# Offsets on VectorE with an early first row, reordered norms and dots, and gate parts on GpSimd in an eight-stage graph and feed-forward kernel

## The chip, the cores and the metric

The kernel runs on one core of a Trainium2 chip. A core has five engines that work side by side, each through its own queue in order: TensorE (PE in the profile; PEld is its weight load), VectorE (DVE), ScalarE (ACT), GpSimd (POOL) and SyncE (SP), which here only issues DMA transfers. An engine waits for another by a semaphore, and whatever stands behind the waiting instruction in its queue waits too. The metric is the time of one execution on the device in microseconds (us); the figure is a median of several runs.

## The reference

`x` holds 625 nodes of 768 numbers. Eight stages each add something to it, four graph layers and four feed-forward layers in turn; every stage reads a layer norm of `x`:

```python
x = x + L0_gnn(layernorm(x))   # graph attention, 12 heads of 64
x = x + L0_ffn(layernorm(x))   # 8 experts, 2 per node, hidden size 192
x = x + L1_gnn(layernorm(x))   # normalised graph convolution
x = x + L1_ffn(layernorm(x))   # attention over all nodes, then 8 experts
x = x + L2_gnn(layernorm(x))   # two graph convolutions
x = x + L2_ffn(layernorm(x))   # soft mixture, 4 experts
x = x + L3_gnn(layernorm(x))   # two graph attention layers, 4 heads and 1
x = x + L3_ffn(layernorm(x))   # 8 experts, 2 per node
```

The attention of a graph layer is, for an edge from `s` to `d`:

```python
e = leaky_relu(a1[s] + a2[d], 0.2)
w = exp(e - max over the edges into d of e)
out[d] = sum(w * h[s]) / sum(w)
```

The first layer of L1_ffn's experts has biases, and its second layer too; all inputs and outputs are 32-bit floats.

## The kernel before

**Layout.** The nodes lie in five tiles of 125 (`NT`, `P`, `TILES`). `x` is kept with nodes on partitions; `xT` is its layer norm turned, features on partitions, in six chunks (`KD`). PSUM, TensorE's output memory, is one pool of four buffers of two banks (`ps`, line 89), through which every product and every transpose goes. The program is written in the order of the stages; the scheduler of the framework then sets each engine's queue, mostly in that order, and pulls later work ahead where it thinks that an engine would wait. So a line that is written later can stand earlier in a queue, and the profile tells which does.

**Strassen's way of multiplying.** Large products are cut into two by two blocks and made from seven products, with sums of blocks made before. `right_sums` (L421 to 439) makes four sums of the right matrix (L435 to L438, called T3, T2, T4 and T1), `left_sums` (L441) five of the left one on POOL, `tile_pair` (L462) runs the seven products for two node tiles, calling `between` after the first two. `half_nodes`, `half_begin` and `half_rest` do the same for the experts' first layer, where the halves are halves of the nodes.

**Norms.** `ln_tile` (L157) makes statistics on DVE (L167, L170), a square root on ACT (L171), a reciprocal (L172) and the scaling (L180) on DVE. `turn_tile` (L182) turns one tile with six transposes (L187) and copies it out on ACT, plainly (L191) or, for L1_ffn's two norms with weights, in six steps (L194). `final(t)` enters tile t's norm and marks it as due to be turned; `turn_due` turns what is due.

**Graph attention.** For each head, `gat_largest` (L553) spreads `a1` as a row over all partitions (L132, five transposes into one PSUM tile) and takes per node the largest over its edges, one DVE step for a tile (L560), with `mb` as mask; it then makes an offset `u` on POOL (L565 to L569). `gat_scores` (L539) makes the scores, on ACT (L547) and POOL (L551). `gat_exp` (L572) spreads `u` as a row, subtracts it from the whole score matrix on DVE (L582) and takes exponentials on ACT (L584). `gather` multiplies by the features (L118 in L0_gnn). `mask_tile` (L525) turns a tile of the counts and makes the mask. L0_gnn's loop (L873 to L902) runs over the heads as a pipeline: in round i the largest of head i, the exponentials of head i-2, `back` of head i-4, `gather` of head i-3 and the scores of head i. `score(i)` first copies head i-1's maxima with ACT (L813). The maxima and offsets have two buffers each (`gat_m`, `gat_u`).

**Experts.** `experts` (L967) runs the first layer in six blocks of two chunks (loop at L1088), and the gates beside it; `gate` (L1038) multiplies a chunk by its gate. In L1_ffn, `gate_parts` (L953) splits the gates into three 16-bit parts, seven DVE steps, needed by the products with the biases in the second layer. `down` (L1107) runs the second layer: tile 0 whole, then two pairs of tiles, t = 1 and t = 3, with the seven products in the order 1, 6, 7, 4, 2, 5, 3. The results of products 1, 6, 2 and 5 go into one PSUM tile (`a1`, `a2`), those of 7, 4 and 3 into another (`b1`, `b2`). After product 1 its result is copied by ACT (L1178) and the norm of tile 0 for the next stage is entered (L1183).

**Dots for a later stage.** L3_gnn needs its weight matrix times two vectors per head. `attention_vectors` (L1318) makes these beside L0_ffn and L1_ffn: each step loads a 128 by 512 piece (`av_w`, two buffers) and runs two DVE dot products (L1355), after a one-element copy (L1354) that puts them behind a given result. `experts` calls `beside(1, ...)` after each of five blocks (L1102), and `down` calls `beside(7, ...)` after the pair t = 1 (L1215): twelve in each of the two layers.

**Narrow products.** `narrow` (L257) multiplies by a few columns: small matmuls (L268), a copy by ACT (L273), five transposes back (L276) and a reduction on DVE (L277). L3_gnn calls it in its first layer's `second` (L2126) and before its second layer (L2191).

Of the kernel before, what the change touches and what calls it, by code (L numbers as in the profile page):

```python
# [9 lines left out]
F32 = mybir.dt.float32  # L10
# [25 lines left out]
class Net:  # L36
# [120 lines left out]
    def ln_tile(self, src, dst, scale=None, st=None, act=False):  # L157


        nc, sp = self.nc, self.small  # L160
        have = st is not None
        if not have:
            st = sp.tile([P, 12], F32, tag="lt_st", name="lt_st", bufs=3)
        mv = sp.tile([P, 2], F32, tag="lt_mv", name="lt_mv", bufs=3)
        rs = sp.tile([P, 1], F32, tag="lt_r", name="lt_r", bufs=3)
        for h in range(0 if have else 2):
            nc.vector.bn_stats(  # L167
                st[:, 6 * h : 6 * h + 6], src[:, h * (D // 2) : (h + 1) * (D // 2)]
            )
        nc.vector.bn_aggr(mv, st)  # L170
        nc.scalar.activation(rs, mv[:, 1:2], AF.Sqrt, bias=self.eps[:P])  # L171
        nc.vector.reciprocal(rs, rs)  # L172
        if scale is not None:
            nc.vector.tensor_tensor(rs, rs, scale, ALU.mult)
        if act:
            nb = sp.tile([P, 1], F32, tag="lt_n", name="lt_n")
            nc.vector.tensor_scalar(nb, mv[:, 0:1], rs, -1.0, ALU.mult, ALU.mult)
            nc.scalar.activation(dst, src, AF.Identity, bias=nb, scale=rs)
            return
        nc.vector.tensor_scalar(dst, src, mv[:, 0:1], rs, ALU.subtract, ALU.mult)  # L180

    def turn_tile(self, src, dst, t, scale=None, bias=None):  # L182
# [10 lines left out]
        for k in range(KD):  # L193
            nc.scalar.activation(  # L194
                dst[:, k, TILES[t]], pv[:, k, :P], AF.Identity,
                bias=bias[:, k : k + 1], scale=scale[:, k : k + 1],
            )
# [59 lines left out]
    def narrow(self, pool, chunks, w, cols, dst):  # L257


        nc, n, few = self.nc, len(chunks), w  # L260
# [13 lines left out]
        pv = self.nv(self.ps(), P, 128)  # L274
        for t in range(NT):
            nc.tensor.transpose(pv[:, t, :], hT[:, TILES[t]], self.ident)  # L276
        nc.vector.tensor_reduce(  # L277
            dst, pv.rearrange("p t (q e) -> p t e q", q=4)[:, :, 0:cols, :], AX.X, ALU.add
        )
# [141 lines left out]
    def right_sums(self, T, q, eng=None):  # L421
# [16 lines left out]
        eng.tensor_tensor(T1, B12, B11, ALU.subtract)  # L438
# [114 lines left out]
    def gat_largest(self, pool, mb, a1, a2):  # L553

        nc = self.nc
        row = self.spread(lambda t: a1[:, t : t + 1], P)
# [8 lines left out]
        nc.gpsimd.tensor_tensor(u, m, a2, ALU.add)  # L565
        v = self.small.tile([P, NT], F32, tag="gat_v", name="gat_v")
        nc.gpsimd.tensor_scalar(v, u, 0.8, 0.0, ALU.mult, ALU.max)
        nc.gpsimd.tensor_scalar(u, m, 0.2, None, ALU.mult)
        nc.gpsimd.tensor_tensor(u, u, v, ALU.add)  # L569
# [17 lines left out]
    def L0_gnn(self):  # L587
# [5 lines left out]
        with ExitStack() as ctx:  # L593
# [196 lines left out]
            for s in range(NT):  # L790
                self.log_counts(lc, s)
            for t in range(NT):
                self.mask_tile(mb, t, act=True)
# [79 lines left out]
            for i in range(H + 4):  # L873
                if i < H:
                    ms[i], us[i] = self.gat_largest(tmpp, mb, a1[i], a2[i])
# [77 lines left out]
    def gate_parts(self, gb, after):  # L953
# [4 lines left out]
        nc.vector.tensor_copy(r[:, 0, 0:1], after)  # L958
        parts = gb[:, :, 0, 0 : 3 * NEXP].rearrange("p t (e i) -> p t e i", i=3)
        nc.vector.tensor_copy(parts[:, :, :, 0], lg)  # L960
        nc.vector.tensor_tensor(r, lg, parts[:, :, :, 0], ALU.subtract)
        nc.vector.tensor_copy(parts[:, :, :, 1], r)
        nc.vector.tensor_tensor(parts[:, :, :, 2], r, parts[:, :, :, 1], ALU.subtract)
        for j in range(1, gb.shape[2]):
            nc.vector.tensor_copy(gb[:, :, j, 0 : 3 * NEXP], gb[:, :, 0, 0 : 3 * NEXP])

    def experts(self, over_all, w1, w2, gelu, b1=None, b2=None, after=None, beside=None):  # L967

        nc, tc, a, x = self.nc, self.tc, self.a, self.x
        with tc.tile_pool(name="moe", bufs=1) as big, ExitStack() as up_pool:  # L970
# [117 lines left out]
            for c in range(2, NF + 2, 2):  # L1088
# [12 lines left out]
                if beside and c < NF:  # L1101
                    beside(1, hg[:P, c + 1, 0:1])  # L1102
# [4 lines left out]
    def down(self, pool, w2, hg, gT, bias, after, beside):  # L1107
# [47 lines left out]
        for t in (1, 3):  # L1155
# [18 lines left out]
            )  # L1174
            U = pool.tile([P, 2, HD], F32, tag="U", name="U")
            U2, U3 = U[:, 0], U[:, 1]
            prod(1, a1)
            nc.scalar.copy(U2, a1)  # L1178
            add(x11, U2)
            prod(6, a2)  # L1180
            add(U2, U2, a2)
            if after and t == 1:
                self.final(0)  # L1183
            prod(7, b1)
            add(U3, U2, b1)
            add(x12, U2)
            prod(4, b2, (t + 1, bl))
# [12 lines left out]
            add(x22, U3)  # L1200
            prod(5, a2, (t + 1, br))
# [3 lines left out]
            add(x12, a2)  # L1205

# [7 lines left out]
            if beside and t == 1:  # L1214
                beside(7, U3[:, 0:1])  # L1215
# [179 lines left out]
    def L1_ffn(self):  # L1395
# [3 lines left out]
        with ExitStack() as ctx:  # L1399
# [31 lines left out]
            rights = self.right_sums(vp, columns(wv))  # L1431
# [570 lines left out]
    def L3_gnn(self):  # L2002
# [5 lines left out]
        with ExitStack() as ctx:  # L2008
# [23 lines left out]
            def project(h, *between):  # L2032
# [13 lines left out]
                for i, t in enumerate((1, 3)):  # L2046
                    if i < len(between):
                        between[i](T)
                    self.tile_pair(
                        T[:P, 3 * HK], lefts[t], rights,  # L2050
                        [hh[h][:, o, c, 0:HH] for o in (t, t + 1) for c in range(2)],
# [74 lines left out]
            def second(T):  # L2126
                self.turn_due(NT - 1)
                self.narrow(tp, [xT[:, k, :] for k in range(KD)], self.v1, 2 * H, ends)
                sums_of(3, None)
                for t in range(3, NT):  # L2130
                    self.mask_tile(mb, t)
# [59 lines left out]
            self.narrow(tp, chs, self.v2, 2, c)  # L2191
# [69 lines left out]
            prod(lambda t: A[t][0], B11, one, (1,))  # L2261
            self.gat_scores(w, c1, self.spread(lambda t: c2[:, t : t + 1], P), lc)
# [134 lines left out]
```

## Time and profile before

| what | us |
|---|---|
| median of 3 runs | 1891.52 (1891.14 to 1892.33) |
| the profiled execution, its own time | 1890.76 |
| its span, first to last instruction | 1889.0 |

| stretch, us from the start | stage | TensorE busy | DVE | ACT | POOL | granted clock |
|---|---|---|---|---|---|---|
| 0 to 90 | L0_gnn, counts of edges | 79.18 | 74.27 | 26.94 | 1.89 | 0.98 |
| 90 to 110 | L0_gnn, masks, first head | 11.98 | 14.89 | 14.89 | 10.63 | 0.74 |
| 110 to 225 | L0_gnn, heads | 96.29 | 103.14 | 99.33 | 94.00 | 0.86 |
| 303 to 344 | L0_ffn, second layer | 37.25 | 30.98 | 3.29 | 23.59 | 0.96 |
| 700 to 730 | L1_ffn, into the experts | 28.49 | 17.38 | 14.61 | 15.22 | 1.00 |
| 730 to 765 | L1_ffn, first layer of experts | 32.50 | 20.15 | 7.41 | 23.66 | 1.00 |
| 790 to 830 | L1_ffn, second layer | 36.57 | 31.74 | 3.04 | 23.59 | 1.00 |
| 1405 to 1452 | L3_gnn, first heads | 44.77 | 29.17 | 12.97 | 24.83 | 1.00 |

The profile comes from one execution. A line of its timeline reads: start in us, length in us, engine, line of the kernel, operation, the tile written and the tiles read with their shapes, how many were merged, and in brackets how long the engine had stood idle before it and what ended that. `128x384 f32` is partitions by elements; `L125` is the helper through which most matmuls go, so the tile names tell the product. Busy time of TensorE is modelled; idle time of an engine that nothing waits for costs nothing.

### The profile page before, as it was taken

How to read it: one execution, taken by the hardware profiler on the slowest of the kernel's cores; microseconds unless marked ns; L12 is line 12 of the kernel's file. 1: busy time of each engine (PE TensorE's matmuls, PEld its weight loads, DVE VectorE, ACT ScalarE, POOL GpSimd, SP SyncE). 2: the span in 40 equal slices, each digit the busy share in tenths (PEclk: the TensorE clock that was granted, in tenths of full speed). 3: DMA queues.
4: the chain of work that ended last, by engine and by line, in shares of the span. 5: the costliest groups of instructions: out<-in, count | busy, mean ns of one | idle time of the engine just before them, and what ended most of it. 6: DMA issues, size and time to landing. Idle time of an engine off the chain costs nothing.

```text
span 1889.0 us, 21692 instructions
## 1 busy us (share of the span) xinstructions
PE 1821.8 (96%) x8224; PEld 1270.4 (67%) x8224; DVE 1112.4 (59%) x2211; ACT 528.2 (28%) x963; POOL 658.4 (35%) x556
## 2 busy tenths in 40 slices
PE   8969899999999999999999999999999999999998
PEld 7844565555677766655555778878767888556765
DVE  8789856547566765674936464555756555144452
ACT  2479721002254533100110131322314233111200
POOL 0079665234410044743106322231235321401551
PEclk9968999999999999999999999999999999999999
DMA  2040142210200024414420211001011122021321
GB/s 70 22 145 34 40 116 70 78 58 27 92 25 26 1 70 153 127 53 140 138 67 34 76 43 59 26 26 34 6 39 35 40 72 67 1 73 52 94 72 33
DMA packets 69637, 115.03 MB, mean 61 GB/s; under 512 B 8189, under 2 KB 38111, under 8 KB 69534
## 3 DMA queue, kind: packets, MB, share of 16 engines
q1 hardware_dynamic: 69274, 113.57, 18.9%
q8 instruction: 65, 1.06, 0.2%
q14 instruction: 38, 0.31, 0.1%
q10 hardware_dynamic: 260, 0.09, 0.0%
HBM read 111.63 MB, written 2.01 MB: 60 GB/s over the span
## 4 chain that ended last, share of the span: by engine, by line
PE 84%; DVE 8%; ACT 2%; DMA 2%; issue 2%; POOL 1%; SPq 0%; ACTq 0%; DVEq 0%; POOLq 0%
PE ps L125 65%; PE ps L118 4%; PE ps L768 2%; PE ps L1889 2%; PE ps L1518 2%; PE ps L1550 2%; PE ps L1537 1%; PE ps L187 1%; POOL gat_w L551 1%; PE ps L132 1%; DVE gat_w L582 1%; PE ps L1735 1%; DMA x<-in_x 1%; PE ps L706 1%; DVE av_junk L1355 1%
## 5 line engine op out<-in xcount | busy, mean ns | idle before, releaser
L327 POOL TENSOR_TENSOR S<-w 128x384 f32<-128x384 f32 x40 | 41.4, 1040 | 401.9 <-PE ps L125 298.9
L125 PE MATMUL ps<-xT,w 128*128 128x313 f32 x480 | 137.6, 427 | 0.7 <-ACT pr L1526 0.7
L125 PE MATMUL ps<-w,xT 128*125 128x384 f32 (+2 forms) x392 | 125.2, 473 | 0.0
L125 PE MATMUL ps<-T,w 128*128 128x313 f32 x408 | 122.0, 430 | 0.9 <-DVE U L401 0.9
L551 POOL TENSOR_TENSOR gat_w<-gat_w,xT 125x625 f32<-125x625 f32 x60 | 86.2, 1469 | 102.8 <-DVE xT L523 96.5
L125 PEld LDWEIGHTS ps<-xT,w 128*128 128x128 f32 x480 | 89.3, 189 | 33.6 <-ACT pr L1526 0.9
L125 PE MATMUL ps<-T,S 128*128 128x313 f32 x348 | 103.8, 432 | 1.7 <-DVE T L307 1.4
L125 PEld LDWEIGHTS ps<-w,xT 128*125 128x125 f32 x392 | 72.8, 188 | 46.2 <-issue 11.1
L125 PE MATMUL ps<-xT,S 128*128 128x313 f32 x336 | 100.9, 429 | 2.1 <-DVE hg L401 2.1
L125 PE MATMUL ps<-w,S 128*125 128x384 f32 x292 | 99.8, 487 | 2.6 <-DVE x L1170 2.6
L125 PEld LDWEIGHTS ps<-T,w 128*128 128x128 f32 x408 | 75.6, 189 | 32.2 <-issue 1.8
L125 PE MATMUL ps<-w,hg 128*125 128x384 f32 x288 | 96.3, 486 | 0.0
L125 PE MATMUL ps<-hh,gat_w 125*125 125x257 f32 (+1 forms) x400 | 89.8, 379 | 0.0
L125 PE MATMUL ps<-w,x2T 128*125 128x384 f32 (+1 forms) x280 | 84.2, 449 | 0.0
L125 PEld LDWEIGHTS ps<-T,S 128*128 128x128 f32 x348 | 64.0, 189 | 28.7 <-ACT lt L355 4.4
L125 PEld LDWEIGHTS ps<-w,S 128*125 128x125 f32 x292 | 54.5, 188 | 42.4 <-DVE x L1170 3.9
L125 PEld LDWEIGHTS ps<-hh,gat_w 125*125 125x125 f32 x400 | 73.4, 187 | 11.3 <-issue 0.4
L125 PEld LDWEIGHTS ps<-xT,S 128*128 128x128 f32 x336 | 62.1, 189 | 26.6 <-POOL hg L1041 2.5
L118 PE MATMUL ps<-gat_w,ft 125*65 125x500 f32 (+1 forms) x240 | 74.9, 471 | 4.4 <-DVE gat_w L582 3.1
L125 PEld LDWEIGHTS ps<-w,hg 128*125 128x125 f32 x288 | 53.6, 188 | 36.6 <-issue 0.6
L1355 DVE CUSTOM_DVE_ANT_0 av_junk<-av_w,av_a 128x512 f32<-128x512 f32 (+1 forms) x80 | 74.1, 926 | 6.4 <-DMA av_w<-in_L_gnn_W 4.1
L560 DVE CUSTOM_DVE_ANT_0 junk<-ps,mb 125x625 f32<-125x625 f32 x85 | 68.5, 806 | 13.9 <-PE ps L132 9.9
(459 smaller groups left out, 3794.7 us busy)
## 6 DMA issues: line engine op xcount, KB each, us to landing
w<-in_L_ffn_phiT SPq DMA_DIRECT2D x8, 1536.0 KB
w<-in_L_gnn_W SPq DMA_DIRECT2D x8, 1536.0 KB
gate<-gD SPq DMA_DIRECT2D x24, 312.5 KB
w<-in_L_ffn_w SPq DMA_DIRECT2D x6, 1152.0 KB
w<-in_L_gnn_W SPq DMA_DIRECT2D x6, 1152.0 KB
av_w<-in_L_gnn_W SPq DMA_DIRECT2D x24, 256.0 KB
av_w<-in_L_gnn_W SPq DMA_DIRECT2D x16, 384.0 KB
w<-in_L_ffn_w SPq DMA_DIRECT2D x3, 1536.0 KB
```

What stands on the lines that cost most here:

```text
L118: self.nc.tensor.matmul(pv[:, s, :], lhs[i], rhs[i][:, s, :], start=i == 0, stop=i == n - 1)
L125: self.nc.tensor.matmul(out, lhs[i], rhs[i], start=i == 0, stop=i == n - 1)
L132: self.nc.tensor.transpose(pv[:, t, :], col(t).to_broadcast([P, rows]), self.ident[:P, :P])
L187: nc.tensor.transpose(pv[:, k, :P], src[:, k * 128 : (k + 1) * 128], self.ident[:P, :P])
L327: nc.gpsimd.tensor_tensor(S1, A21, A22, ALU.add)
L551: nc.gpsimd.tensor_tensor(w[:, s, :], w[:, s, :], lc[:, s, :], ALU.add)
L560: nc.vector.tensor_tensor_reduce(self.n3(junk), row, self.n3(mb[:, t, :]), 1.0, -3e38, ALU.subtract, ALU.max, m[:, t : t + 1],)
L768: nc.tensor.matmul(acc[j // 2][:, j % 2, :], ohs[:, TILES[j]], ohd[:, 0:HN], start=c == cs[0], stop=c == cs[-1],)
L1355: nc.vector.tensor_tensor_reduce(junk, wt, row, 1.0, 0.0, ALU.mult, ALU.add, dst)
L1518: nc.tensor.matmul(sv[r][:, s, :], qk[half[r], 0, TILES[t]], self.n3(qk[half[r], 1, :])[:, s, :], start=True, stop=True,)
L1550: nc.tensor.matmul(ov[half[r]], v[:, s, h * DH : (h + 1) * DH], pT[r][:, s, :], start=s == 0, stop=s == NT - 1,)
L1889: nc.tensor.matmul(pv[:, j, :], zTs[t][:, k, :], w2[k // 3][:, k % 3, js], start=k == 0, stop=False,)
```

## The change

Several small edits are made together. (1) The offset `u` is made by two DVE steps in place of four on POOL, in all 17 heads: `0.2 m + max(0.8 (m + a2), 0)` becomes the equal `max(0.2 m, m + 0.8 a2)`. (2) In L0_gnn the row for head 0 is spread before the masks. (3) In `down`, two one-column ACT copies put the square root of tile 0's norm behind the copy of product 1. (4) The seven dots steps after the pair t = 1 are dealt out: two more among the first layer's blocks, one at the end of the pair t = 1, four in the pair t = 3. (5) `gate_parts` goes from DVE to POOL. (6) The last sum of L1_ffn's value weights goes to POOL. (7) When the last tile is turned with weights, every second chunk is written by DVE. (8) The transposes of both narrow products, and the two last masks of L3_gnn, move behind matmuls.

```diff
 def ln_tile(...)
         nc.vector.bn_aggr(mv, st)
+        if behind is not None:
+            nc.scalar.copy(rs, behind)
         nc.scalar.activation(rs, mv[:, 1:2], AF.Sqrt, bias=self.eps[:P])
 def turn_tile(...)
         for k in range(KD):
+            if t == NT - 1 and k % 2:
+                nc.vector.tensor_scalar(
+                    dst[:, k, TILES[t]], pv[:, k, :P], scale[:, k : k + 1], bias[:, k : k + 1],
+                    ALU.mult, ALU.add,
+                )
+                continue
 def narrow(...)
-        pv = self.nv(self.ps(), P, 128)
-        for t in range(NT):
-            nc.tensor.transpose(pv[:, t, :], hT[:, TILES[t]], self.ident)
-        nc.vector.tensor_reduce(
-            dst, pv.rearrange("p t (q e) -> p t e q", q=4)[:, :, 0:cols, :], AX.X, ALU.add
-        )
+        def turned():
+            pv = self.nv(self.ps(), P, 128)
+            for t in range(NT):
+                nc.tensor.transpose(pv[:, t, :], hT[:, TILES[t]], self.ident)
+            nc.vector.tensor_reduce(
+                dst, pv.rearrange("p t (q e) -> p t e q", q=4)[:, :, 0:cols, :], AX.X, ALU.add
+            )
+        return turned
 def right_sums(self, T, q, eng=None, last=None)
-        eng.tensor_tensor(T1, B12, B11, ALU.subtract)
+        (last or eng).tensor_tensor(T1, B12, B11, ALU.subtract)
 def gat_largest(self, pool, mb, a1, a2, row=None)
-        row = self.spread(lambda t: a1[:, t : t + 1], P)
+        if row is None:
+            row = self.spread(lambda t: a1[:, t : t + 1], P)
...
-        nc.gpsimd.tensor_tensor(u, m, a2, ALU.add)
-        v = self.small.tile([P, NT], F32, tag="gat_v", name="gat_v")
-        nc.gpsimd.tensor_scalar(v, u, 0.8, 0.0, ALU.mult, ALU.max)
-        nc.gpsimd.tensor_scalar(u, m, 0.2, None, ALU.mult)
-        nc.gpsimd.tensor_tensor(u, u, v, ALU.add)
+        nc.vector.scalar_tensor_tensor(u, a2, 0.8, m, ALU.mult, ALU.add)
+        nc.vector.scalar_tensor_tensor(u, m, 0.2, u, ALU.mult, ALU.max)
 def L0_gnn(self)
             for s in range(NT):
                 self.log_counts(lc, s)
+            row = self.spread(lambda t: al[:, t, 0, 0:1], P)
             for t in range(NT):
                 self.mask_tile(mb, t, act=True)
...
-                    ms[i], us[i] = self.gat_largest(tmpp, mb, a1[i], a2[i])
+                    ms[i], us[i] = self.gat_largest(
+                        tmpp, mb, a1[i], a2[i], None if i else row
+                    )
 def gate_parts(self, gb, after)
-        nc.vector.tensor_copy(r[:, 0, 0:1], after)
+        nc.gpsimd.tensor_copy(r[:, 0, 0:1], after)
...
 def experts(...)
                 if beside and c < NF:
-                    beside(1, hg[:P, c + 1, 0:1])
+                    beside(2 if c in (4, 8) else 1, hg[:P, c + 1, 0:1])
 def down(...)
+            def dots(n, after):
+                if beside and n in ((5,) if t == 1 else (1, 2, 3, 4)):
+                    beside(1, after[:, 0:1])
             prod(1, a1)
             nc.scalar.copy(U2, a1)
+            if after and t == 1:
+                nc.scalar.copy(U3[:, 0:1], U2[:, 0:1])
             add(x11, U2)
+            dots(1, x11)
             prod(6, a2)
             add(U2, U2, a2)
+            dots(2, U2)
             if after and t == 1:
-                self.final(0)
+                self.final(0, behind=U3[:, 0:1])
             prod(7, b1)
             add(U3, U2, b1)
             add(x12, U2)
+            dots(3, x12)
...
             add(x22, U3)
+            dots(4, x22)
             prod(5, a2, (t + 1, br))
             add(x22, a2)
...
             add(x12, a2)
+            dots(5, x12)
...
-            if beside and t == 1:
-                beside(7, U3[:, 0:1])
 def L1_ffn(self)
-            rights = self.right_sums(vp, columns(wv))
+            rights = self.right_sums(vp, columns(wv), last=nc.gpsimd)
 def L3_gnn(self)
                 for i, t in enumerate((1, 3)):
+                    behind = None
                     if i < len(between):
-                        between[i](T)
+                        behind = between[i](T)
                     self.tile_pair(
                         T[:P, 3 * HK], lefts[t], rights,
-                        [hh[h][:, o, c, 0:HH] for o in (t, t + 1) for c in range(2)],
+                        [hh[h][:, o, c, 0:HH] for o in (t, t + 1) for c in range(2)], behind,
                     )
...
             def second(T):
                 self.turn_due(NT - 1)
-                self.narrow(tp, [xT[:, k, :] for k in range(KD)], self.v1, 2 * H, ends)
+                turned = self.narrow(tp, [xT[:, k, :] for k in range(KD)], self.v1, 2 * H, ends)
                 sums_of(3, None)
-                for t in range(3, NT):
-                    self.mask_tile(mb, t)
+                def behind():
+                    turned()
+                    for t in range(3, NT):
+                        self.mask_tile(mb, t)
+                return behind
...
-            self.narrow(tp, chs, self.v2, 2, c)
+            turned = self.narrow(tp, chs, self.v2, 2, c)
...
             prod(lambda t: A[t][0], B11, one, (1,))
+            turned()
             self.gat_scores(w, c1, self.spread(lambda t: c2[:, t : t + 1], P), lc)
```

## The prediction, made before the changed kernel was run

> **What bounds the kernel now.** I read the page's first part, then the chain of waits, then TensorE's own waits, then the timeline around each of those.
>
> ```profile
> PE 1821.8 (96%) x8224; PEld 1270.4 (67%) x8224; DVE 1112.4 (59%) x2211; ACT 528.2 (28%) x963; POOL 658.4 (35%) x556
> ...
> PE 84%; DVE 8%; ACT 2%; DMA 2%; issue 2%; POOL 1%; SPq 0%; ACTq 0%; DVEq 0%; POOLq 0%
> ```
>
> TensorE is busy 1821.8 of 1889.0 us and carries 84% of the chain. The change removes no matmul, so it can only win out of the 67.2 us in which TensorE stands. Who it stands for (engine, line, waited for: us in total, times, longest):
>
> ```profile
> PE ps L132 <- POOL gat_u L569: 10.1, 3, 6.2
> PE ps L125 <- ACT U L1178: 5.0, 2, 2.6
> ...
> PE ps L125 <- DVE x L1170: 2.6, 2, 1.5
> ...
> PE ps L125 <- DVE hg L401: 2.1, 1, 2.1
> PE ps L276 <- ACT narrow L273: 1.6, 2, 0.8
> PE ps L125 <- DVE T L307: 1.4, 3, 0.9
> ...
> PE ps L187 <- DVE xn L180: 1.3, 1, 1.3
> ```
>
> From L0_ffn on TensorE is nearly full, so a wait taken from it there is time taken off. L0_gnn (90 to 225 us) is different: TensorE is busy 108.3 of 135 us and four engines hand work round; a wait of TensorE there is worth something only if the loop behind it gets shorter. I cost each part at its own place.
>
> **First head of L0_gnn (row spread ahead of the masks, offsets on DVE).** Timeline:
>
> ```profile
> 99.11 9.50 POOL L551 TENSOR_TENSOR gat_w<-gat_w,xT 125x625 f32<-125x625 f32 x5 [96.53 <-DVE xT L523]
> ...
> 109.52 0.20 POOL L569 TENSOR_TENSOR gat_u<-gat_u,gat_v 125x5 f32<-125x5 f32 x1
> ...
> 111.26 3.41 DVE L582 TENSOR_TENSOR gat_w<-gat_w,ps 125x3125 f32<-125x3125 f32 x1 [0.95 <-POOL gat_w L551]
> ```
>
> The four little POOL steps of head 0 (L565 to L569, 108.58 to 109.72) wait behind five L551; then TensorE spreads them (1.37) and L582 starts. The maxima (L560) start at 103.84 because the row is spread after the five masks. With the row first, each maximum waits only for its mask: ACT makes them every 1.37 us, the last at 105.6, so the fifth maximum ends at about 106.5. Two DVE steps of 5 columns cost about 0.35 (L844, also 125x5, is 0.19 long and lets the next start after 0.11). Spread done by 108.5; then L582 waits only for POOL's L551, 108.6. Start 108.75 instead of 111.26: **-2.5**. ACT's exp, the later rows and the gathers hang on L582, so they come along. The masks lose one of four PSUM buffers to the row; mask 3 then waits for ACT's release of mask 0 (100.9) and ACT reaches it only at 103.48: nothing.
>
> **Offsets in the other heads.** One head lasts 8.70 us (L582 at 159.05, 167.75, 176.45), in a ring:
>
> ```profile
> 166.02 0.78 PE L132 MATMUL ps<-ident,gat_u 125*125 125x125 f32 x5 [1.30 <-DVE gat_m L560]
> ...
> 166.70 0.18 ACT L813 COPY gat_w<-gat_m 125x5 f32<-125x5 f32 x1
> ...
> 167.01 0.81 DVE L560 CUSTOM_DVE_ANT_0 junk<-ps,mb 125x625 f32<-125x625 f32 x1 [0.56 <-POOL gat_u L565]
> ...
> 167.75 3.40 DVE L582 TENSOR_TENSOR gat_w<-gat_w,ps 125x3125 f32<-125x3125 f32 x1
> ```
>
> ACT's exps, L826, L813, one maximum, L582, exps again. POOL's offsets are not in it, so taking four steps (1.1 us) off POOL gains nothing. But `gat_u` has two buffers: the offset of head i overwrites that of head i-2, just read by the spread at 166.02. POOL could wait for that; now DVE waits, with L560 and L582 queued behind it and ACT's exps behind those. Behind L582 the two steps are free; between L560 and L582 they add 0.35 in each of some ten heads. The 0.56 idle lies in front and swallows part: I take **+0.8**, ends -1 (where POOL's late offset held a spread, as at 126.28) and +3.5.
> Can TensorE itself get faster here? The granted clock is 0.86 over 110 to 225 us: 20 gather matmuls take 7.18 at 119.77, after a stall of 6.2, and 5.43 in later heads. The Trainium skill ("TensorE: Matmul & The Clock Gate", Part 1) says that the clock halves after about 3.4 us of idleness, so a stall pushed below that would give 1.7 more. But the first stall goes from 6.2 to about 5 (from 109.9, when the first spread and the next row are out, to 115, when head 1's offset is there), still cold by the rule; I count 0.
>
> **Norm of tile 0 in both down-products.** Timeline of L0_ffn:
>
> ```profile
> 320.71 0.81 PE L125 MATMUL ps<-Td,hg 128*125 128x384 f32 x2
> ...
> 323.24 0.29 ACT L171 ACTIVATE lt_r<-lt_mv,eps 125x1 f32<-125x1 f32 x1 [18.50 <-DVE lt_mv L170]
> ...
> 323.63 0.48 ACT L1178 COPY U<-ps 125x384 f32<-125x384 f32 x1
> ...
> 324.17 5.83 PE L125 MATMUL ps<-Td,S 128*125 128x384 f32 x12 [2.64 <-ACT U L1178]
> ```
>
> The first product ends at 320.7; its copy could run at once, but ACT's queue has the norm's square root (L171) in front, which waits for DVE. TensorE stands 2.64 (and 2.31 in L1_ffn). The two one-column copies force the square root behind the L1178 copy: copy at 320.9, done at 321.4, when TensorE has just done its two filler matmuls. The price is two ACT copies of 0.19 (as L906), with nothing behind them but the norm of a tile turned 9 us later. Next late would be T2 and S2, ready by 313.5 and 311. **-4.5** of 4.95.
>
> **Dots.** Seven pairs (one 0.14 copy, two of 0.77) leave the end of pair t=1. There they ran with DMA waits of 1.18 and 1.38 in DVE's queue, and TensorE stood 1.53 (344.42) and 1.12 (829.31) for an L1170 sum behind them: **-2.4** of 2.65. Four now run in t=3, each behind a sum with a product of 3.9 us before the next read is due; DVE is idle 15 us between 356 and 380. Each has two `av_w` buffers and some 8 us for a 256 KB load; SP's queue sends the next stage's weights after them, so that load moves from 355.0 to about 362, needed at 379.7. Two more pairs per FFN go among the up-products at c = 4 and 8. There TensorE already stood 0.46 and 0.42 for a sum wedged between dots: cost 0 if they fit into DVE's gaps (2.2 us per block), 1.5 each if not; **+0.6** in all, ends 0 and 6.
>
> **L1_ffn.** (1) The fourth subtraction of the value weights goes to POOL. L438 took 1.34 at 459.14, ahead of the last tile's norm, and TensorE waited 1.28 for its xn at 463.77: **-1.2**. On POOL it costs about 2.7 (1.77 for 768 columns at L435, times 1.5), in a queue idle from 458.8 to 463.7; its product starts at 468.3. DVE may pay too: L180, the norm's scaling, took 1.10 beside a POOL step at 458.11 and 0.68 without one. A rule speaks against the move: the Trainium skill ("SBUF — State Buffer", SBUF: two separate sides) has DVE and GpSimd share a port pair that one of them holds for a whole instruction. By the rule L180 could wait the full 2.7, and the part would lose 1.4; by the row it loses 0.4 at most. POOL is through at 461.5, before the last L180 is due (461.7): I keep -1.2. (2) Half of tile 4's affine turn on DVE: six ACT steps take 2.19 at 722.74, then the T sums wait and TensorE 0.87. Three on each engine take 1.1: **-0.9**; at 464.6 nothing waits for it. (3) The gates' parts: DVE's five steps, L961 to L965, held L401 from 748.29 to 751.30 (L961 alone 1.49 for 40 columns), and TensorE stood 2.05 at 751.91: **-1.9**. POOL pays about 2.2 for seven steps of 0.2 to 0.4 (L1054, L567), where it has gaps of 2.05 and 1.09; behind them stand the gate multiplications, and sums used 11 us later.
>
> **L3_gnn.** Both narrow products' transposes move behind matmuls, so their ACT copy (0.83 and 0.80) is covered. The second now has DVE's reduction (0.2 and its hand-over) straight before the spread that reads it: -0.8 and -0.4. The offset at 1450.42 waits no more: -0.5. Masks 3 and 4 come 2.6 later and hold the logarithms (ACT L522, 1426.7 to 1429), which have until 1435: +0.2. **-1.5**.
>
> **Sum.** -2.5 + 0.8 - 4.5 - 2.4 + 0.6 - 1.2 - 0.9 - 1.9 - 1.5 = **-13.5 us**. The profiled execution took 1890.76 (span 1889.0, 1.76 around it), so it would take 1877.3; the median of the runs lies 0.76 higher, at 1891.52: **1878.0**.
>
> **Rivals.** Less than 0.2% (3.8 us) counts as no change.
> - *Waits reappear* (0.25): in the FFNs the freed waits come back as shorter ones for the next sum. For it: TensorE's products in one PSUM tile wait for each other's reads (prod 6 for L1178), so any late DVE read shows. Against: the covers counted above. Half of the 10.9 from the FFN parts: 1883.4.
> - *L0's ring lengthens* (0.13): offsets land between maximum and L582 in all heads and the first head's gain is lost in reordering: 1878.0 + 2.7 + 2.5 = 1883.2; with 0.5 lost per head more, 1888.
> - *Dots in the product chain* (0.10, the other side): 14 pairs move between products, 1.68 each. If each holds the read that the next product waits for, 14 x 1.68 = 23.5 comes against 14.1 of gains (13.5 and the 0.6 already counted): 1901. It is slower than before once more than 8 of 14 are uncovered. For it: the 0.4 waits among the up-products; against: the seven in a row cost only 1.5.
> - *The change doesn't do it* (0.04): the square root, gates or dots keep their places in the queues: 1891.
>
> **Numbers.** My forecast has 0.48 (1873 to 1882). Faster by over 0.2%: 0.48 + 0.25 + 0.10 of the ring = 0.83; within: 0.06; slower: 0.11. The range 1867 to 1888 takes in -1 and +3.5 for the ring, 0 to 6 for the dots and all waits gone (1874), some luck in order below that, and both milder rivals; it leaves out the dots' rival and no effect.
>
> **What would show it.** L582 first starting at about 108.8; no wait of TensorE for L1178, gat_u or the L401 at 751.9; the last norm's wait under 0.2; heads of 8.7 to 9.0 us. I am wrong if heads last over 9.2, if new waits for L1170 or L401 sum to over 5, or if TensorE waits for POOL in L1_ffn.

## The result and the profile after

| | us |
|---|---|
| median before, same chip (5 runs) | 1891.52 (1890.98 to 1892.68) |
| median after (5 runs) | 1898.54 (1898.24 to 1900.42) |
| after to before | 1.0038, 95% interval 1.0023 to 1.0053 |
| the profiled execution after, and its span | 1898.24, 1896.5 |

The change makes the kernel 7.0 us slower, where 13.5 us of gain were forecast. The page of the changed kernel, busy times and then the chain of waits by engine:

```profile
PE 1821.6 (96%) x8224; PEld 1270.7 (67%) x8224; DVE 1143.8 (60%) x2251; ACT 526.9 (28%) x961; POOL 652.3 (34%) x496
...
PE 85%; DVE 7%; ACT 3%; DMA 2%; issue 1%; POOL 1%; SPq 0%; DVEq 0%; ACTq 0%; POOLq 0%
```

TensorE's busy time is as before; its idle time went from 67.2 to 74.9 us. DVE's busy time grew by 31 us although its dots are as many as before: some of it is the offsets, some is steps that last longer (the 80 dots alone take 84.2 for 74.1). TensorE's own waits in the changed kernel (engine, line, waited for: us in total, times, longest):

```profile
PE ps L125 <- DVE U L414: 16.3, 6, 6.4
...
PE ps L132 <- DVE gat_u L582: 9.0, 2, 6.0
...
PE ps L125 <- DVE T L320: 1.4, 3, 0.9
PE ps L125 <- DVE U L1187: 1.3, 2, 0.9
```

Line numbers have moved: L414 is L401 of before (the sums of the experts' first layer), L1187 is L1170, L582 makes the offset, L595 is the large subtraction (L582 before), L1383 the dots (L1355), L1372 the load of their tile. The waits for L1178, for the `hg` sum, for `narrow` and for the last norm are gone, as forecast. In their place stands one new line: 16.3 us for the `U` sum, 0.9 before. (The spread of head 0's and head 1's offsets waits for DVE now, and hardly less than it waited for POOL; the matmuls behind the split turn, second line from the end, wait 0.9 as before.) The new wait is neither in the second layer nor behind a DMA by name; DVE's timeline at c = 4 in L0_ffn shows what holds it:

```profile
268.93 0.16 DVE L1382 COPY av_junk<-hg 125x1 f32<-125x1 f32 x1 [0.26 <-ACT hg L1037]
269.12 0.84 DVE L1383 CUSTOM_DVE_ANT_0 av_junk<-av_w,av_a 128x512 f32<-128x512 f32 x1
...
270.00 1.36 DVE L1383 CUSTOM_DVE_ANT_0 av_junk<-av_w,av_a 128x512 f32<-128x512 f32 x1
...
274.04 1.14 DVE L1383 CUSTOM_DVE_ANT_0 av_junk<-av_w,av_a 128x512 f32<-128x512 f32 x1 [2.67 <-DMA av_w<-in_L_gnn_W]
...
275.11 0.47 DVE L398 TENSOR_TENSOR hg<-U,ps 128x313 f32<-128x313 f32 x1
275.50 1.59 DVE L1383 CUSTOM_DVE_ANT_0 av_junk<-av_w,av_a 128x512 f32<-128x512 f32 x1
...
277.02 0.47 DVE L414 TENSOR_TENSOR U<-U,ps 128x313 f32<-128x313 f32 x1
```

The second pair stands *ahead* of the U sum. DVE waits 2.67 for the pair's tile, then needs 3 us for it, and the sum that ran at 272.8 in the kernel before runs at 277.0. In the kernel before, the gap of DVE lay behind that sum:

```profile
272.80 0.48 DVE L401 TENSOR_TENSOR U<-U,ps 128x313 f32<-128x313 f32 x1
275.38 0.48 DVE L401 TENSOR_TENSOR hg<-U,ps 128x313 f32<-128x313 f32 x1 [2.10 <-PE ps L125]
```

TensorE's timeline in the changed kernel, at c = 4 of L0_ffn and then of L1_ffn:

```profile
270.09 2.80 PE L125 MATMUL ps<-T,S 128*128 128x313 f32 x10
277.64 3.47 PE L125 MATMUL ps<-T,w 128*128 128x313 f32 x6 [4.75 <-DVE U L414]
...
766.34 3.47 PE L125 MATMUL ps<-T,w 128*128 128x313 f32 x6 [6.42 <-DVE U L414]
```

In L0_ffn it stands 4.75 us, because product 7 goes into the PSUM tile whose other half this sum reads, and then runs six matmuls in 3.47 us that take 1.74 elsewhere: the granted clock is 0.50 there. So the price of a stall can be more than its length.

The same matmul can be found in both profiles, and the difference of its starts followed along the kernel. That gives the account of the whole change in the two profiled executions:

| place | after against before, us | forecast |
|---|---|---|
| L0_gnn to its end (both parts) | -0.7 | -1.7 |
| second pairs, L0_ffn: c = 4, c = 8 | +6.4, +2.5 | +0.3 |
| second pairs, L1_ffn: c = 4, c = 8 | +8.2, +3.9 | +0.3 |
| U copy ahead of the root, both layers | -3.9, -2.2 | -4.5 |
| dots away from the end of t = 1, and a new wait of 0.86 at t = 3 | -2.1, -1.3, +0.9 | -2.4 |
| last subtraction to POOL | -1.5 | -1.2 |
| half of the turn on DVE | +0.6 | -0.9 |
| gates' parts to POOL | -2.2 | -1.9 |
| L3_gnn | -1.1 | -1.5 |
| sum | +7.5 (spans: +7.5) | -13.5 |

The second pairs make +21.0 of it; all the rest together makes -13.5. Of the -0.7 of L0_gnn, 0.6 was there at 80 us, before any changed line ran, so its two parts together gave 0.1 and not 1.7.

### The profile page after: what moved, and what is told of

Same layout as the page of the kernel before. It is cut to its first block, busy times and chain, and to the rows that moved or that the text cites. A ratio compares the mean times of both kernels' runs of the same rounds, so it can differ in the third digit from the quotient of the medians.

```text
span 1896.5 us, 21647 instructions
## 1 busy us (share of the span) xinstructions
PE 1821.6 (96%) x8224; PEld 1270.7 (67%) x8224; DVE 1143.8 (60%) x2251; ACT 526.9 (28%) x961; POOL 652.3 (34%) x496
## 4 chain that ended last, share of the span: by engine, by line
PE 85%; DVE 7%; ACT 3%; DMA 2%; issue 1%; POOL 1%; SPq 0%; DVEq 0%; ACTq 0%; POOLq 0%
PE ps L125 66%; PE ps L118 4%; PE ps L781 2%; PE ps L1917 2%; PE ps L1546 2%; PE ps L1578 2%; PE ps L1565 1%; PE ps L189 1%; DVE gat_w L595 1%; DMA av_w<-in_L_gnn_W 1%; DVE av_junk L1383 1%; PE ps L1763 1%; ACT gat_w L597 1%; PE ps L132 1%; DMA x<-in_x 1%
## 5 line engine op out<-in xcount | busy, mean ns | idle before, releaser
L125 PE MATMUL ps<-T,w 128*128 128x313 f32 x408 | 126.5, 442 | 16.3 <-DVE U L414 16.3
L125 PE MATMUL ps<-xT,w 128*128 128x313 f32 x480 | 137.6, 427 | 0.7 <-ACT pr L1554 0.7
L125 PE MATMUL ps<-w,xT 128*125 128x384 f32 (+2 forms) x392 | 125.3, 473 | 0.0
L125 PEld LDWEIGHTS ps<-xT,w 128*128 128x128 f32 x480 | 89.4, 189 | 33.8 <-ACT pr L1554 0.9
L125 PEld LDWEIGHTS ps<-T,w 128*128 128x128 f32 x408 | 77.3, 194 | 49.6 <-issue 20.9
L125 PE MATMUL ps<-T,S 128*128 128x313 f32 x348 | 104.8, 435 | 1.7 <-DVE T L320 1.4
L125 PEld LDWEIGHTS ps<-w,xT 128*125 128x125 f32 x392 | 72.8, 188 | 46.4 <-issue 11.3
L125 PE MATMUL ps<-xT,S 128*128 128x313 f32 x336 | 100.8, 429 | 0.0
L125 PE MATMUL ps<-w,S 128*125 128x384 f32 x292 | 99.2, 486 | 0.0
L125 PE MATMUL ps<-w,hg 128*125 128x384 f32 x288 | 96.5, 487 | 0.0
L125 PE MATMUL ps<-hh,gat_w 125*125 125x257 f32 (+1 forms) x400 | 89.8, 379 | 0.0
L1383 DVE CUSTOM_DVE_ANT_0 av_junk<-av_w,av_a 128x512 f32<-128x512 f32 (+1 forms) x80 | 84.2, 1052 | 7.1 <-DMA av_w<-in_L_gnn_W 5.1
L125 PEld LDWEIGHTS ps<-T,S 128*128 128x128 f32 x348 | 64.8, 192 | 29.4 <-ACT lt L368 4.4
L125 PE MATMUL ps<-w,x2T 128*125 128x384 f32 (+1 forms) x280 | 84.3, 450 | 0.0
L125 PEld LDWEIGHTS ps<-hh,gat_w 125*125 125x125 f32 x400 | 73.3, 187 | 11.3 <-issue 0.4
L125 PEld LDWEIGHTS ps<-w,S 128*125 128x125 f32 x292 | 54.7, 188 | 39.0 <-issue 0.7
L125 PEld LDWEIGHTS ps<-w,hg 128*125 128x125 f32 x288 | 53.9, 189 | 36.8 <-issue 0.9
L125 PEld LDWEIGHTS ps<-xT,S 128*128 128x128 f32 x336 | 62.1, 189 | 24.2 <-DVE lt L360 1.8
L781 PE MATMUL ps<-ohd,ohs 125*125 125x313 bf16 x425 | 65.1, 308 | 9.7 <-DVE ohs L774 9.7
```

The lines of the kernel that those rows point to most:

```text
L125: self.nc.tensor.matmul(out, lhs[i], rhs[i], start=i == 0, stop=i == n - 1)
L781: nc.tensor.matmul(acc[j // 2][:, j % 2, :], ohs[:, TILES[j]], ohd[:, 0:HN], start=c == cs[0], stop=c == cs[-1],)
L1383: nc.vector.tensor_tensor_reduce(junk, wt, row, 1.0, 0.0, ALU.mult, ALU.add, dst)
```

## Experiments

My theory: the second pairs are the loss, by their place ahead of the U sum. The products of the experts' first layer are called up-products here, those of the second down-products. Rivals: dots cost DVE's time wherever they stand; or POOL, which got the gates' parts, is what makes DVE late. Each run is compared with the kernel before on the same chip; the medians of before were 1891.38 to 1891.70. Where two variants differ by 1 us, their runs overlap and the profile has to speak.

### The second pairs moved to the second layer (e1)

```diff
-beside(2 if c in (4, 8) else 1, hg[:P, c + 1, 0:1])
+beside(1, hg[:P, c + 1, 0:1])
-if beside and n in ((5,) if t == 1 else (1, 2, 3, 4)):
+if beside and n in ((4, 5) if t == 1 else (1, 2, 3, 4, 5)):
```

> The changed kernel with one pair of dots behind each block of up-products (c = 4 and 8 as the others) and the two freed pairs among the down-products (behind products 4 to 5 at t=1, one more at t=3). Theory (the doubled pairs hold DVE's queue ahead of the U read, TensorE stands 4.8, 2.1, 6.4 and 2.2 us for it and restarts at a lower clock): matching TensorE's matmuls one by one between the two profiles, the changed kernel falls behind by 6.4 + 2.5 us at these two places of L0_ffn and by 8.2 + 3.8 in L1_ffn, 20.9 together; they go, the moved pairs cost about 1: 1878.5, 1876 to 1882, U L414 waits under 1.5 in sum. Rival 1 (the dots cost their DVE time wherever they stand): waits for U L1187 grow instead, 1890 or more. Rival 2 (the gates' parts and the gates on POOL make DVE late in L1_ffn, not the pairs): the two waits of L1_ffn stay above 4 in sum, 1886 to 1890.

Measured: 1876.83 (1876.06 to 1877.30), ratio to before 0.9922 (0.9907 to 0.9936). TensorE's waits in this run:

```profile
PE ps L125 <- DVE U L1187: 1.2, 2, 0.8
PE ps L125 <- DVE U L414: 1.1, 3, 0.4
```

The 21.7 us between this and the changed kernel are the price of four pairs' place. The seven pairs that now lie among the second layer's products cost no more than five did (L1187: 1.2 against 1.3). The first rival falls.

### The second pairs alone, on the kernel before (e2)

```diff
-beside(1, hg[:P, c + 1, 0:1])
+beside(2 if c in (4, 8) else 1, hg[:P, c + 1, 0:1])
-beside(7, U3[:, 0:1])
+beside(5, U3[:, 0:1])
```

> The kernel before with only this: two pairs of dots instead of one at c = 4 and 8, five instead of seven at the end of t=1. Theory (doubled pairs alone make the loss): +20.9 and about -1 for two pairs fewer at the end: 1911, 1906 to 1914, with four waits of 2 us and more for U L401. Rival (the loss needs the change's other parts, as the gates' parts on POOL): in L1_ffn the waits stay under 2 in sum, 1895 to 1902. If the doubled pairs are not the cause: 1890 to 1893.

Measured: 1906.09 (1905.39 to 1909.27), 1.0080 (1.0065 to 1.0095): 14.6 us slower, in the direction and by most of the size, but at the low edge. In the profiled execution, the slowest of the four (1909.27), the waits for U sum to 11.6, not 16.3:

```profile
PE ps L125 <- DVE U L401: 11.6, 6, 4.7
```

At c = 4 of L1_ffn TensorE stood 1.8 here, and 6.4 in the changed kernel. So something in the rest of the change makes that one place dearer: the second rival has a part.

### The gates' parts back on DVE, second pairs kept (e5)

```diff
 def gate_parts(...)
-nc.gpsimd.tensor_copy / tensor_tensor
+nc.vector.tensor_copy / tensor_tensor
```

> The changed kernel with the gates' parts in L1_ffn back on DVE, as before; doubled pairs stay. Interaction theory (the parts on POOL hold POOL's gate multiplications, so SP's queue sends the third weight tile later, the reduction waits 1.54 for it and the next one, 4.21 instead of 1.08, falls beside POOL's bias parts): the wait for U at c = 4 in L1_ffn falls from 6.4 to about 2, its cold restart (1.65) goes, the 2 us wait at the parts returns: 1898.5 - 6.1 + 2.1 = 1894.5. Rival (the parts' place doesn't matter to the pairs): the 6.4 stays and 2.1 is added: 1900.6.

Measured: 1893.01 (1890.94 to 1897.33), 1.0013 (1.0005 to 1.0022): 5.5 faster than the changed kernel, by undoing an edit that gains. The wait at c = 4 fell from 6.4 to 1.8 and the one at the parts came back, as expected. The reason that I gave is wrong, though. SP issues the weight tile at 753.01 here and at 753.59 in the changed kernel, so POOL's queue did not delay it. What differs is when DVE asks: the first dot of c = 4 starts at 760.13 here, at 756.24 there. In the changed kernel DVE at that place, then POOL beside it:

```profile
760.46 0.80 DVE L1383 CUSTOM_DVE_ANT_0 av_junk<-av_w,av_a 128x512 f32<-128x512 f32 x1 [1.54 <-DMA av_w<-in_L_gnn_W]
...
761.58 4.21 DVE L1383 CUSTOM_DVE_ANT_0 av_junk<-av_w,av_a 128x512 f32<-128x512 f32 x1
```

```profile
761.37 0.82 POOL L1072 CAST b2p<-b2t 96x768 bf16<-96x768 f32 x1
762.15 1.50 POOL L1058 TENSOR_TENSOR hg<-hg,gate 128x625 f32<-128x625 f32 x1
763.61 1.63 POOL L1073 TENSOR_TENSOR b2t<-b2t,b2p 96x768 f32<-96x768 f32 x1
```

With the parts' stall gone, the kernel reaches c = 4 some 4 us sooner, ahead of a tile that lands no sooner. DVE waits 1.54 for it, and the next dot then falls beside these three POOL steps and lasts 4.21, where it is 0.69 with POOL idle and 1.08 in this run.

### Four buffers for the tile (e3)

```diff
-wt = pool.tile([128, cols], F32, tag="av_w", name="av_w", bufs=1 + which)
+wt = pool.tile([128, cols], F32, tag="av_w", name="av_w", bufs=4 if which == 1 else 3)
```

> The changed kernel with four buffers instead of two for the weight tile of the dots in the FFNs (three as before elsewhere); pairs as in the changed kernel. If the DMA decides (the third reduction at c = 4 waits 2.67 and 1.54 for its tile): these waits go, the stalls at c = 4 fall from 4.75 and 6.42 to 2.1 and 4.9, the cold restart of the first (1.65) goes too: 1891 to 1894. If DVE's own time decides (four reductions of 0.7 to 4.2 ahead of the U read): the waits turn into little, 1896 to 1899. The stalls at c = 8 (2.1 and 2.2) have no DMA wait and stay by both.

Measured: 1885.67 (1885.20 to 1887.73), 0.9969 (0.9958 to 0.9981): 12.9 less than the changed kernel, more than either theory gave. DVE in L1_ffn at c = 4 in this run:

```profile
754.59 1.36 DVE L1383 CUSTOM_DVE_ANT_0 av_junk<-av_w,av_a 128x512 f32<-128x512 f32 x1
...
756.27 1.08 DVE L1383 CUSTOM_DVE_ANT_0 av_junk<-av_w,av_a 128x512 f32<-128x512 f32 x1
...
757.28 0.47 DVE L414 TENSOR_TENSOR U<-U,ps 128x313 f32<-128x313 f32 x1
```

No DMA wait, so the dot is through before POOL's long bias steps begin (757.46), and the 4.21 goes with it; I had left that in the sum. TensorE's waits for U are 9.3, none above 2.5. The remaining distance to the version with the pairs moved, 1885.67 - 1876.83 = 8.8, is what the pairs' own DVE time ahead of the sum costs. So, with the pairs in this place, 12.9 of the 21.7 us hang on the late tile (wait, collision with POOL, restarts at a low clock) and 8.8 are left for the place alone.

### The second pair behind the U sum (e6 and e11)

```diff
 def rest(c, *between):
+    if beside and c in (6, 10):
+        u = begun[c]
+        between = (lambda: beside(1, u[:P, 0:1]), *between[1:])
...
-beside(2 if c in (4, 8) else 1, hg[:P, c + 1, 0:1])
+beside(1, hg[:P, c + 1, 0:1])
```

> The changed kernel, as many pairs among the up-products (seven per FFN), but the second pair of c = 4 and of c = 8 stands behind the next block's U read instead of ahead of it. Place theory (what costs is only what stands ahead of the read that product 7 waits for): TensorE's waits for U L414 fall from 16.3 to under 2: 1877 to 1880, as with the pairs moved to the down-products. Load theory (one pair more per block is too much for DVE or for the tile's DMA among the up-products, wherever it stands): waits for the later sums (hg L414) of 1 to 2 each at four places, 1882 to 1888.

The same with four buffers:

> The kernel with the second pair behind the U read (seven pairs among the up-products), with four buffers for the weight tile. In the run with two buffers the reductions waited 0.86 and 0.63 for the tile and then fell beside POOL's steps (1.80, 1.87 and 4.25 instead of 0.69), and TensorE waited 2.27 and 3.65 for the sums behind them. If the DMA begins it: no DMA wait, reductions of 1.4 at most, TensorE's waits under 1 each: 1877 to 1879. If POOL alone makes it: the reduction beside POOL's bias parts still takes over 3, TensorE's waits stay over 4 in sum: 1881 to 1883.

Measured: with two buffers 1883.02 (1878.00 to 1884.91), 0.9952 (0.9939 to 0.9965); with four 1876.33 (1875.47 to 1878.04), 0.9922 (0.9909 to 0.9934). With two, the waits for U are down to 0.8, which is the place theory's; but the late tile is still there, at c = 4 of both layers (TensorE's waits for the `hg` sum are 5.9 in two). DVE in L1_ffn, two buffers; L1386 is the line of the dots here:

```profile
752.73 0.69 DVE L1386 CUSTOM_DVE_ANT_0 av_junk<-av_w,av_a 128x512 f32<-128x512 f32 x1 [0.63 <-DMA av_w<-in_L_gnn_W]
...
753.47 4.25 DVE L1386 CUSTOM_DVE_ANT_0 av_junk<-av_w,av_a 128x512 f32<-128x512 f32 x1
```

and with four:

```profile
750.55 1.15 DVE L1386 CUSTOM_DVE_ANT_0 av_junk<-av_w,av_a 128x512 f32<-128x512 f32 x1
...
751.75 0.69 DVE L1386 CUSTOM_DVE_ANT_0 av_junk<-av_w,av_a 128x512 f32<-128x512 f32 x1
```

Behind a wait of 0.63 for a tile, the next step took 4.25 instead of 0.69. With the pair behind the sum and the tile in time, seven pairs among the up-products cost no more than five: 1876.33 against 1876.83. That settles both halves of the cause, but not one split between them:

| second pairs | two buffers | four buffers |
|---|---|---|
| ahead of the U sum | 1898.54 | 1885.67 |
| behind it | 1883.02 | 1876.33 |

The buffers are worth 12.9 ahead of the sum and some 6.7 behind it (the six runs at 1883.02 spread over 7 us); the place is worth some 15.5 with two buffers and 9.3 with four. Each half makes the other dearer.

### The root ahead of the copy again (e8)

```diff
-    if after and t == 1:
-        nc.scalar.copy(U3[:, 0:1], U2[:, 0:1])
-        self.final(0, behind=U3[:, 0:1])
+    if after and t == 1:
+        self.final(0)
```

On top of the version with the pairs moved.

> The pairs moved to the down-products (as the first run), but without the two one-column copies, so that the square root of tile 0's norm may stand ahead of the copy of U on ACT again. If only the waits count (2.64 and 2.31 before): 1876.8 + 4.9 = 1881.7. If the restart at a lower clock counts too (matmuls behind the wait of 2.64 lost another 1.3 against the changed kernel, those behind 2.31 nothing): 1883. If the copies do nothing: 1876.8.

Measured: 1882.08 (1880.46 to 1883.83), 0.9948 (0.9935 to 0.9961): 5.3 more than with the copies. The waits for the copy of U, `PE ps L125 <- ACT U L1200` in this run, are back at 5.0 in two. The medians lie between "waits only" (4.9) and "waits and one slow restart" (6.2); in the profiled execution, the slowest of its runs, the matmuls behind both waits ran slow for a while.

### Later heads' offsets on POOL (e4 and e7)

```diff
 def gat_largest(...)
+    if first:
         nc.vector.scalar_tensor_tensor(u, a2, 0.8, m, ALU.mult, ALU.add)
         nc.vector.scalar_tensor_tensor(u, m, 0.2, u, ALU.mult, ALU.max)
+        return m, u
+    nc.gpsimd.tensor_tensor(u, m, a2, ALU.add)
+    ...
```

On top of the pairs moved: first with only head 0 of L0_gnn on DVE, then with head 0 and all of L3_gnn.

> As e1, and the offsets of all heads but the first of L0_gnn (and those of L3_gnn) back on POOL as in the kernel before; the first head keeps its early row and its DVE offset. Theory (two DVE steps per head lie in the ring: starts of the large subtraction are 8.60 and 9.48 apart in turn, 18.07 for two heads, against 17.40 before): heads of 8.70 again, and about 2.5 to 3 less than e1: 1875.5. Rival (the first gain is given back for another reason, as the later heads' order on ACT): within 1 of e1.

> The pairs moved to the down-products (as the first run), offsets of L0_gnn's later heads on POOL, those of the first head and of L3_gnn on DVE. From the two profiles: nine heads from the first large subtraction to the last take 84.5 with the offsets on DVE, 82.5 on POOL, of which 0.5 is lost again by the end of L0_gnn; L3_gnn loses 1.0 with the offset on POOL. So 1876.8 - 2.0 + 0.5 = 1875.3, and 82.5 between the first and the last subtraction. If the ring is not what sets L0_gnn's end: 1876.8.

Measured: 1875.80 (1875.12 to 1877.54), 0.9918 (0.9903 to 0.9933), and 1875.63 (1875.04 to 1877.23), 0.9917 (0.9904 to 0.9930). From the first large subtraction to the tenth, nine heads take 82.6 us before, 84.0 in the changed kernel, 84.5 with the pairs moved, 82.5 and 82.6 in these two. In all thirteen profiles it is 83.7 to 84.8 with the later offsets on DVE and 81.7 to 82.6 with them on POOL. So the two DVE steps do lengthen the ring, by 1.0 at least; of that about 1 reaches the end of the kernel, less than the 2.5 to 3 that I expected, and the medians alone do not prove it.

### The turn (e9 and e10)

On top of the last version: all six steps on ACT, or columns 4 and 5 on DVE.

```diff
-if t == NT - 1 and k % 2:
-    nc.vector.tensor_scalar(...)
-    continue
```

> The version with the pairs in the down-products and the later heads' offsets on POOL, with all six steps of the last tile's affine turn on ACT, as before. In the changed kernel the three steps of each engine take turns (each waits 0.2 to 0.5 for the other's; 724.32 to 727.09, 2.77 us, against 2.19 for six on ACT), and TensorE's router matmuls fall 0.5 behind there. So this should gain 0.5 in L1_ffn and at most as much at the other turn: 1875.1, hardly to be told by the median; in the profile the turn takes 2.2 and TensorE's lag at the router goes. If the split helps: 1876.5.

```diff
-if t == NT - 1 and k % 2:
+if t == NT - 1 and k >= 4:
```

> As e9, but columns 0 to 3 of the turn on ACT and 4 and 5 on DVE: these two lie in the second half of the PSUM tile. If the turns are taken because both engines read the same half, the two run beside each other now: 4 x 0.37 = 1.5 us in all, 1.3 less than in the changed kernel, 1874.3. If they are taken because both write one tile, DVE starts behind ACT's fourth: 1.5 + 0.2 + 0.7 = 2.4, 1875.2.

Measured: 1874.57 (1873.68 to 1876.39), 0.9914 (0.9900 to 0.9927), and 1875.33 (1874.37 to 1875.75), 0.9914 (0.9901 to 0.9928). In the changed kernel the two engines alternate, without the matmuls and weight loads between:

```profile
724.32 0.46 ACT L202 ACTIVATE xT<-ps,column 128x125 f32<-128x125 f32 x1 [0.22 <-PE ps L189]
...
724.81 0.41 DVE L197 TENSOR_SCALAR xT<-ps,column 128x125 f32<-128x125 f32 x1 [0.20 <-ACT xT L202]
...
725.25 0.46 ACT L202 ACTIVATE xT<-ps,column 128x125 f32<-128x125 f32 x1 [0.47 <-DVE xT L197]
```

Each waits for the other, and the six steps take 2.77 us; all on ACT they take 2.19. With columns 4 and 5 on DVE, ACT's four steps end at 715.32 and DVE's two start at 715.47, 2.37 in all:

```profile
715.00 0.55 DVE L320 TENSOR_TENSOR T<-xT 128x378 f32<-128x378 f32 x1 [0.89 <-ACT xT L202]
715.47 0.72 DVE L197 TENSOR_SCALAR xT<-ps,column 128x125 f32<-128x125 f32 x2
```

This is the time expected if the engines take turns because they write one tile, but it does not show that. In DVE's queue a T sum (L320), which itself waits for ACT's steps, stands ahead of the two and keeps DVE until they start; the other turn of this run has the same order. So whether the turns come from the half of the PSUM tile read or from the tile written stays open.

## Why the prediction was wrong

**The step that failed** is "Two more pairs per FFN go among the up-products at c = 4 and 8 ... cost 0 if they fit into DVE's gaps (2.2 us per block), 1.5 each if not; +0.6 in all, ends 0 and 6". They cost 21.7. Three things were wrong in it.

1. *The gap lay on the wrong side.* DVE's 2.2 us of idleness in a block come behind the U sum (at 272.8 before, idle until 275.4). The pair was issued ahead of it, where the first pair had already used the slack up: the waits of 0.46 and 0.42 that I quoted said so. Worth 8.8 us for four pairs with the tile in time, more with it late.
2. *A transfer was not followed.* With two buffers the third tile can be asked for only when the second dot of an earlier pair is done. In L0_ffn that is at 263.48; SP, behind loads of gates, issues it at 266.28, and it lands at 274.04 where the pair wants it at 271.4. I followed such a load for the pairs at t = 3 and not for these. Worth, with what hangs on it, 12.9 us where the pairs stood.
3. *The price of one was taken from a calm place.* 1.5 each was a pair of dots. A dot is 0.69 long alone, 0.8 to 1.9 beside POOL's sums and gates, 4.2 beside three of its steps in a row, and TensorE came back from the two longest stalls at half clock (+1.7 each).

The rival that was nearest is *Dots in the product chain*, at 0.10. Its mechanism is the right one, a dot ahead of the read that the next product waits for. Its numbers are not: it had 14 pairs at 1.68 each and more than 8 of them uncovered; 4 pairs were uncovered, at 5.4 each. Of the signs that I set, "new waits for L1170 or L401 sum to over 5" came.

**The other steps**, by the account above and the runs:

- *First head*: -2.5 expected with the large subtraction's start at 108.75. It started at 109.69, 1.6 earlier than before, of which 0.6 was there before this part began: the part gave 1.0. The maxima came as I said (the fifth ended at 105.9, which is 106.5 less the same 0.6). The two offset steps were taken at 0.35 together and took 2.15: 0.68 and 0.82 beside POOL's multiplications, with a maximum of the next head between them.
- *Ring*: +0.8 expected, +1.4 measured, inside its range. Heads are 8.60 and 9.48 long in turn. The line about 9.2 was crossed by every second head, not by their mean of 9.0.
- *U copy*: -4.5 expected; -6.1 in the account, and undone it gives back 5.3. Right, and short by a restart at the low clock.
- *Dots at the end of t = 1*: -2.4 expected, -2.5 in the account; a new wait of 0.86 for L1187 took what went beyond.
- *Last subtraction*: -1.2, measured -1.5. TensorE does not wait for that xn any more. But POOL was not through before the last norm's scaling, as I had it: its subtraction took 2.94, from 461.79 to 464.73, and the scaling, at 464.11, took 1.04 instead of 0.68. So 0.4 of the rule on the shared port, weighed there, shows on DVE, not the full length of POOL's step.
- *Half of the turn*: -0.9 expected, +0.6 measured. I added up two engines' halves as if they ran beside each other; they take turns.
- *Gates' parts*: -1.9, measured -2.2, and then more than taken back while the second pairs stood behind them.
- *L3_gnn*: -1.5, measured -1.1.

Apart from the second pairs the sum was right: 1878.0 less their 0.6 is 1877.4, and the kernel without them measures 1876.83. In the account the single errors against the forecast (first head +1.5, turn +1.5, ring +0.6, U copy -1.6) cancel in large part, which is luck and no merit of the steps. The fastest version here has the pairs in the second layer, the later offsets of L0_gnn on POOL and the turn on ACT: 1874.57, 0.9914 (0.9900 to 0.9927) of before; its distance to the versions next to it, about 1 us, is within the spread of their runs.

## What to carry to other kernels

When work is put into a gap of an engine, find out between which two instructions of its queue the gap lies and on which side of the time-critical read the new work is issued; an idle sum per block says neither. Follow the new work's transfer as well: when its buffer comes free, what is ahead of it in the issuing queue, when it lands; and do it again for the schedule after the change, because a stall removed upstream makes the same transfer late. Several edits measured as one number hide each other: here -13.5 and +21.0 were one +7.5.

## What the runs showed of the hardware

**A stall's length does not tell whether the clock drops.** TensorE behind a wait of 2.04 in the run with the gates' parts on DVE:

```profile
753.98 2.36 PE L125 MATMUL ps<-xT,S 128*128 128x313 f32 x4 [2.04 <-DVE hg L414]
```

and behind one of 3.65 in the run with the pair behind the U sum and two buffers:

```profile
758.17 1.32 PE L125 MATMUL ps<-xT,S 128*128 128x313 f32 x4 [3.65 <-DVE hg L414]
```

The same four matmuls take 2.36 after the short stall and 1.32 after the long one; the granted clock is 0.51 from 754 to 757 in the first and 1.00 from 758.2 to 760 in the second. In the record of the clock the spells at half speed last 3.41 us or a multiple of it, and within an execution all changes lie on one grid of 3.41 us. The Trainium skill ("TensorE: Matmul & The Clock Gate", Part 1) has a free-running window of about that length and the clock halved after one idle window. On the grid, the stall of 3.65 lay across two windows, with 1.98 in one and 1.67 in the next. The stall of 2.04 lay in one window, 750.64 to 754.05, and the half speed began at its end. So a window need not be wholly idle, and the page's rule is too mild here: 1.98 in a window left the clock at full speed, 2.04 halved it.

The other profiles agree. From 230 us on, behind L0_gnn, the thirteen profiles have 15 windows at full speed in which TensorE, by its modelled busy time, stood 2.04 us or more, and half speed followed each of them; it followed none in which TensorE stood 1.98 or less. In L0_gnn, with its smaller matmuls, half speed also followed windows with 1.2 to 1.9 of standing, so the standing time alone is not the whole rule. For a forecast this means that a stall pushed just below 3.4 us can still cost the restart.

**A DVE step can wait for several POOL steps, not for one.** The dots of 4.21 and 4.25 began beside one POOL step and ended 0.5 to 0.6 behind the second that came after it. The skill ("SBUF — State Buffer", SBUF: two separate sides) says that a DVE step with two inputs in SBUF and a POOL step that reads SBUF exclude each other for a whole instruction. Here DVE lost to three in a row, so 1.5, the length of one POOL step, is no upper bound for what such a step can lose.
